# A two-layer network on one core: attention with a shift of 48 and fewer pieces, table sends without an order among themselves, and the last two tiles in two banks

## The chip, the core and the metric

The kernel runs on one core of a Trainium2 chip. The engines of a core work beside one another, each through its own list of instructions in order: TensorE (PE: matrix products; PEld is its weight load), VectorE (DVE), ScalarE (ACT), GpSimd (POOL), and SyncE (SP), which here only issues transfers. Transfers are carried out by the core's DMA engines; SP and GpSimd issue nearly all of them. The metric is the device time of one execution in microseconds (us); the kernel before takes 1606.64 us, the median of three runs (1605.18 to 1611.37).

## The reference, cut to what matters

Two layers work on 2 x 2048 tokens of 256 numbers. The first layer is a gated linear attention beside a quantised product. The second, which the change is about, is a softmax attention with 16 heads of 16 numbers and a bias that falls with distance, beside a layer of 8 experts of which each token goes through two:

```python
slopes = 1.0 / (24.0 ** (1.0 / 8)) ** jnp.arange(1, 9)      # 0.67 down to 0.042
fwd = slopes * jnp.tril(rel) + jnp.triu(neg, 1)             # heads 0..7: keys at or before the query
bwd = slopes * jnp.triu(-rel) + jnp.tril(neg, -1)           # heads 8..15: keys at or after it
scores = jnp.einsum('bhqd,bhkd->bhqk', q, k) / sqrt(16) + bias
out = jnp.einsum('bhqk,bhkd->bhqd', softmax(scores), v) @ Wf + bf
...
pi = _sinkhorn(-logits)                                     # 20 rounds over 8 experts
_, top_idx = jax.lax.top_k(pi, 2)
y = W_down[e] @ (silu(W_gate[e] @ x) * (W_up[e] @ x))       # 256 -> 1024 -> 256
out = sum of y[top_idx[k]] * pi[k] over k                   # x is the normalised row
```

Each head's slope is the same in both directions: heads h and h + 8 have the same one.

## The kernel before

All matrix products are in float32. After the first layer (`layer0`, until 433.7 us of the profiled execution) come two stages, and the change touches both.

**Attention** (`attention`). Keys lie on partitions and queries in columns. Queries come in tiles of 256 (`QT`), keys in tiles of 128. Heads lie in places: four places form a group, whose four heads sit in the four row groups of 32 partitions, so that four small products run beside each other. `PLACES` says which head has which place; groups 0 and 1 hold the forward heads (way 0), groups 2 and 3 the backward ones (way 1). A part is one batch, way, query tile and group, and parts follow one another by batch, then way, then in the order of `ORDERS`, both groups each time. The operands of groups 0 to 3 lie in the buffers `qk0` to `qk3`.

A fixed number, `SHIFT`, takes the place of the row's maximum: it stands as a row of the query operand (`_bias_rows`), so that a score comes out with bias and shift in it and ScalarE takes the exp of it directly. A score without bias is at most 16 (`LIMIT`). A key so far away that 16 less the shift less slope times distance is under -104 has an exp of 0 in float32, and pieces beyond that distance are left out:

```python
reach = math.ceil((104 + LIMIT - SHIFT) / slope) + 1
```

`_units` makes a list of all pieces (one head, one tile of keys, up to 256 queries, widths in multiples of 32) and packs it into units: each of the four row groups is filled up to 512 columns (`WIDE`) with pieces of its head, and goes on to the next part when its own is done, though never more than two parts ahead of the slowest. The loop at the end of `attention` goes through the units. For each it issues the score products (`scores`, L1827), one exp for each row group (L1833), the masks of the diagonal pieces of the unit before (`keep_only`, on VectorE), and the weighted sums of the unit two before (`weighted_sums`, L1847). When a part has ended its sums are copied out of PSUM, and small steps (`normalise`) transpose, divide, project and add; they are taken one in each unit. When a half of 1024 queries is through in both ways, SP stores it to the output (L1819).

**The routing** runs beside it, one step of VectorE work in a unit: the Sinkhorn rounds, the two best experts of every token, and the place of every token in a table in DRAM that is sorted by expert. Then `Routing.sends` writes the table: sixteen times a load of 256 normalised rows and four indirect sends of 128 rows from GpSimd (`Routing.scatter`, L2180). The sends write one tensor, so each waits until the one before has landed. `BEGIN` (32) units before the end of the list the first row loads (`Block.load_rows`, from SP) and weight gathers (L2208, from GpSimd) are issued.

**Experts** (`Experts.pieces`). 32 blocks of 256 rows of the table are computed one after the other. A block's gate and up weights take the room of `qk0`, `qk1` or `qk3` of the attention, its down weights that of `qk2` or of two exp buffers. `open_rows` transposes the rows; for block 0 this is placed four units before the attention ends. `hidden` makes 8 tiles of the 1024 hidden numbers (L2268), and `add_rows` the output of the block: two tiles of 128 rows, 8 products each (L2284), both in one bank of PSUM, then for each tile the weight and bias on VectorE and an indirect send that adds the rows to the output (L2293). These sends write one tensor too and go one after the other. A block's `add_rows` comes one block later, only the last one has nothing behind it.

The order on each engine is not the program's alone: a scheduler places every instruction that has not been held in the program's order by `keep_in_program_order`.

Of the kernel before, what the change touches and what calls it, by code (L numbers as in the profile page):

```python
# [60 lines left out]
ALU = mybir.AluOpType  # L61
# [3 lines left out]
P = 128  # L65
B, N, E = 2, 2048, 256
NT = B * N // P
TPB = N // P
ST = 512
# [5 lines left out]
NG = H1 // 4  # L75


PLACES = (0, 1, 2, 3, 7, 6, 5, 4, 8, 11, 10, 9, 15, 12, 13, 14)
QT = 256

ORDERS = ((6, 7, 2, 3, 0, 1, 4, 5), (1, 0, 5, 4, 7, 6, 3, 2))
WIDE = 512
CENTER = N // 2
NEG_INF = -1.0e9
# [1 line left out]
NFC = FF // P  # L86
# [11 lines left out]
GROWTH, TINY = 1e3, 1e-24  # L98
SPAN = 60.0
LIMIT = 16.0  # L100
SHIFT = 18.0
BEGIN = 32
LATE = 2
KR = HD + 5
# [4 lines left out]
class InOrder:  # L109


    def __init__(self, tc, engine):
        self.tc, self.engine = tc, engine
# [112 lines left out]
@with_exitstack  # L226
def two_layers(ctx: ExitStack, tc: tile.TileContext, a: dict, out: bass.AP):
    nc = tc.nc
    const = ctx.enter_context(tc.tile_pool(name="const", bufs=1))

    def load(name, shape, view=None, eng=None, dt=F32):
        t = const.tile(shape, dt, tag=name, name=name)
        (eng or nc.sync).dma_start(out=t, in_=view if view is not None else a[name])
        return t

    c = SimpleNamespace()
# [24 lines left out]
    c.x_in = a["x"].rearrange("b n e -> (b n) e").rearrange("(t p) e -> p t e", p=P)  # L261
    c.out_v = out[0 : B * N, :].rearrange("(t p) e -> p t e", p=P)

    usual_way(tc, a, out, c)

    def where(flag):
        return tc.If(nc.values_load(flag[0:1, 0:1], min_val=0, max_val=1) > 0)

    with where(c.special):
        with where(c.more):  # L270
            layer1_experts(tc, a, out, c, range(FULLS, NFULL), range(GROUPS, NSMALL // 4))
        with where(c.general):
            general_way(tc, a, out, c)


@with_exitstack
def usual_way(ctx, tc, a, out, c):
    nc = tc.nc
    keep = ctx.enter_context(tc.tile_pool(name="keep", bufs=1))
    acc = keep.tile([P, NT, E], F32, tag="acc", name="acc")  # L280
    la = keep.tile([P, NT, NE], F32, tag="la", name="la")
    norms = keep.tile([P, 1, NSTRIP], F32, tag="norms", name="norms")
    spans = keep.tile([P, NSTRIP, HG, 4, 2], F32, tag="spans", name="spans")
    operands = Operands(nc, keep, a, c)
    ready = Constants(nc, keep, a, c)

    fill = Fill(nc, keep, a, out, c)

    def besides(s):

        if s == 0:
            fill.begin()
            operands.make_first()
            ready.load()
        elif s < NSTRIP - 2:
            fill.rows(s - 1, NSTRIP - 3)
# [7 lines left out]
    routing = Routing(nc, vector, later, a, c)  # L304
    attention(tc, a, out, acc, la, norms, spans, c, operands, ready, routing, vector)


@with_exitstack
def general_way(ctx, tc, a, out, c):
    nc = tc.nc  # L310
    keep = ctx.enter_context(tc.tile_pool(name="gkeep", bufs=1))
    acc = keep.tile([P, NT, E], F32, tag="acc", name="acc")
    xn2T = keep.tile([P, 2, B * N], F32, tag="xn2T", name="xn2T")
    la = keep.tile([P, NT, NE], F32, tag="la", name="la")
    general_layer0(tc, a, acc, xn2T, la, c)
    later = ctx.enter_context(tc.tile_pool(name="glater", bufs=1))
    fill = Fill(nc, later, a, out, c)
    fill.begin()
    fill.rows(0, 1)
    routing = Routing(nc, nc.vector, later, a, c)  # L320
# [1639 lines left out]
class Routing:  # L1960

    def __init__(self, nc, vector, pool, a, c):
        self.nc, self.vector, self.a, self.c = nc, vector, a, c
# [210 lines left out]
    def scatter(self, rows, s):  # L2176

        for n in range(2):
            for to in self.places:
                self.nc.gpsimd.indirect_dma_start(  # L2180
                    out=self.c.table, in_=rows[:, n, :], in_offset=None,
                    out_offset=bass.IndirectOffsetOnAxis(
                        ap=to[:, 2 * s + n : 2 * s + n + 1], axis=0
                    ),
                )

    def sends(self, pool):

# [8 lines left out]
class Block:  # L2197
# [24 lines left out]
    def load_rows(self):  # L2222
# [5 lines left out]
            ),  # L2228
        )
        self.e.tc.keep_in_program_order(load)  # L2230

    def load(self):
        self.load_gate_up()
# [41 lines left out]
            if f % 2:  # L2275
                yield

    def add_rows(self):
        nc, out = self.e.nc, self.e.out
        ps = self.e.rooms("y_ps", self.n, [P, NC * E]).rearrange("p (c d) -> p c d", c=NC)  # L2280
        y = self.e.rooms("y", self.n, [P, NC, E])
        for c in range(self.tiles):
            for fc in range(NFC):
                nc.tensor.matmul(  # L2284
                    ps[:, c, :], lhsT=self.hT[:, fc, c * P : (c + 1) * P], rhs=self.wd[:, fc, :],
                    start=fc == 0, stop=fc == NFC - 1,
                )
        for c in range(self.tiles):
            nc.vector.scalar_tensor_tensor(  # L2289
                y[:, c, :], ps[:, c, :], self.wt[:, c : c + 1], self.e.c.half_bias,  # L2290
                ALU.mult, ALU.add,
            )
            nc.gpsimd.indirect_dma_start(  # L2293
                out=out, out_offset=bass.IndirectOffsetOnAxis(ap=self.to[:, c : c + 1], axis=0),
                in_=y[:, c, :], in_offset=None, compute_op=ALU.add,
            )


class Group:
# [114 lines left out]
class Experts:  # L2414
# [3 lines left out]
    def __init__(self, tc, a, out, c, rooms, blocks, groups):  # L2418
# [5 lines left out]
        for g in groups:  # L2424
# [2 lines left out]
                self.between.append((at, step))  # L2427
            at += 1

    def pieces(self, begun=False):  # L2430


# [20 lines left out]
                between.popleft()[1]()  # L2453
            yield
        if todo:
            todo[-1].add_rows()
        for _, step in between:
            step()

# [181 lines left out]
```

## Time and profile before

| what | value |
|---|---|
| three runs | 1605.18, 1606.64, 1611.37 us |
| the profiled execution: time, span | 1616.2 us, 1614.4 us |
| granted clock of TensorE, mean | 0.987 |
| busy: TensorE, VectorE, ScalarE, GpSimd | 1553.3, 709.9, 689.8, 406.9 us |
| score matmuls, weighted-sum matmuls | 3916 and 3916 |
| exps of the attention (L1833) | 687 |
| sends to the table, first and last start | 64, 611.8 and 842.6 us |
| idle time of GpSimd before them, for a landing | 143.9 us |

The profile is of one execution. Times in it count from its first instruction. A matmul of the program is two in the trace. "Busy" is the time in which an engine has at least one instruction under way; matmuls overlap, so that the start of one burst to the start of the next is the better measure of what a burst costs. In a row of groups there stand line, engine, operation, output and inputs, shapes and count; after the bar the busy time and the mean time of one in ns; after the second bar the engine's idle time before them and what ended it. In a window row there stand the window, its length, for each engine busy time and count, then the granted clock, the DMA engines' share and GB/s.

### The profile page before, as it was taken

The page shows a single profiled execution, that of the slowest core. Times are in us where ns is not written, and L with a number is a line of the kernel's source. Part 1 is how long each engine was busy: PE and PEld are TensorE (multiplying, and loading weights), DVE is VectorE, ACT ScalarE, POOL GpSimd, SP SyncE. Part 2 cuts the span into 40 slices and gives each one's busy share as a digit, 9 for nine tenths or more (in the row PEclk, how much of TensorE's full clock was granted, in tenths as well). Part 3 has the DMA queues.
Part 4 walks back from the last instruction along what each step waited for, and adds up shares of the span by engine and source line. Part 5 has one row for each costly group of instructions (what it writes and reads, how often), then busy time and mean ns, then how long its engine had stood idle before and what let it go on. Part 6 is the DMA issues. An engine that isn't in the chain of part 4 may idle for free.

```text
span 1614.4 us, 32726 instructions
## 1 busy us (share of the span) xinstructions
PE 1553.3 (96%) x13652; PEld 1253.0 (78%) x13652; DVE 709.9 (44%) x2199; ACT 689.8 (43%) x1434; POOL 406.9 (25%) x367
## 2 busy tenths in 40 slices
PE   7789999999999999999999999999999999999995
PEld 4557676676688887887777888888888888888885
DVE  6787776664378867435345222212221221222121
ACT  5454554654586777787877211111121111111110
POOL 4342222212200003234320122232223322232221
PEclk9899999999999999999999999999999999999998
DMA  8810111313450402622215655585756857576521
GB/s 248 216 38 31 55 54 43 94 35 87 143 78 2 85 3 82 145 62 88 79 58 200 245 183 183 183 284 169 240 163 219 258 184 252 166 235 199 174 25 20
DMA packets 84590, 214.19 MB, mean 133 GB/s; under 512 B 8880, under 2 KB 64432, under 8 KB 71984
## 3 DMA queue, kind: packets, MB, share of 16 engines
q0 software_dynamic: 27392, 148.16, 28.9%
q1 hardware_dynamic: 55936, 62.66, 14.5%
q8 instruction: 109, 1.79, 0.5%
q10 hardware_dynamic: 1104, 1.18, 0.2%
q14 instruction: 49, 0.40, 0.1%
HBM read 161.65 MB, written 50.31 MB: 131 GB/s over the span
## 4 chain that ended last, share of the span: by engine, by line
PE 66%; DVE 1%; DMA 0%; issue 0%; ACT 0%; POOL 0%; POOLq 0%
PE h_ps L2268 27%; PE y_ps L2284 14%; PE sc L1827 10%; PE o_ps L1847 9%; PE f_ps L1811 2%; PE o_tr L1784 1%; PE h_ps L2357 1%; PE x_ps L2246 1%; PE on_tr L1803 1%; PE h_ps L2392 0%; DVE pt L117 0%; DMA out<-va,to 0%; DVE o_sb L117 0%; PE h_ps L2380 0%; POOL out L2293 0%
## 5 line engine op out<-in xcount | busy, mean ns | idle before, releaser
L2268 PE MATMUL h_ps<-va,qk 128*128 128x256 f32 x2048 | 448.6, 379 | 0.0
L2268 PEld LDWEIGHTS h_ps<-va,qk 128*128 128x128 f32 x2048 | 388.1, 190 | 57.0 <-issue 4.5
L1833 ACT ACTIVATE pt<-sc 128x512 f32<-128x512 f32 (+3 forms) x687 | 350.5, 597 | 105.1 <-issue 39.7
L2273 ACT ACTIVATE sg<-h_ps 128x256 f32<-128x256 f32 x256 | 98.3, 384 | 530.2 <-PE h_ps L2268 517.0
L2274 DVE TENSOR_TENSOR larger<-sg,h_ps 128x256 f32<-128x256 f32 x256 | 107.9, 421 | 343.7 <-ACT sg L2273 324.6
L1827 PE MATMUL sc<-qk 32*128 32x128 f32 (+6 forms) x3916 | 219.6, 334 | 1.8 <-PE norm_ps L539 1.1
L1827 PEld LDWEIGHTS sc<-qk 32*128 32x128 f32 x3916 | 181.1, 185 | 36.5 <-issue 20.5
L1847 PE MATMUL o_ps<-pt,va 128*32 128x128 f32 (+6 forms) x3916 | 188.6, 319 | 5.9 <-DVE o_sb L117 5.9
L1847 PEld LDWEIGHTS o_ps<-pt,va 128*32 128x32 f32 x3916 | 140.6, 110 | 36.2 <-DVE o_sb L117 7.6
L2293 POOL DMA_INDIRECT out<-va,to x64 | 101.9, 1592 | 182.8 <-DVE larger L2274 55.5
L117 DVE TENSOR_TENSOR pt<-pt,keepmask 128x128 f32<-128x128 f32 (+3 forms) x546 | 118.8, 277 | 61.8 <-ACT pt L1833 61.4
L2284 PE MATMUL y_ps<-qk,larger 128*128 128x256 f32 x512 | 113.8, 379 | 0.1
L2289 DVE SCALAR_TENSOR_TENSOR va<-y_ps,wt,half_bias 128x256 f32<-128x256 f32 x64 | 28.0, 479 | 194.5 <-PE y_ps L2284 194.5
L2284 PE MATMUL y_ps<-larger 128*128 128x256 f32 x512 | 113.2, 379 | 0.0
L2180 POOL DMA_INDIRECT table<-rows,place x64 | 63.3, 989 | 182.5 <-DMA table<-rows,place 143.9
L2284 PEld LDWEIGHTS y_ps<-larger 128*128 128x128 f32 x512 | 96.2, 190 | 12.5
L2284 PEld LDWEIGHTS y_ps<-qk,larger 128*128 128x128 f32 x512 | 95.8, 190 | 12.7 <-DVE larger L2274 0.5
L2208 POOL DMA_INDIRECT qk<-in_wgateup,wrow x32 | 31.7, 989 | 141.3 <-PE h_ps L2268 133.8
L539 PE MATMUL vf_ps<-qk,xnT 128*128 128x512 f32 x128 | 57.9, 605 | 0.0
L117 DVE COPY o_sb<-o_ps 128x256 f32<-128x256 f32 x64 | 26.9, 422 | 51.9 <-PE o_ps L1847 42.7
L539 PEld LDWEIGHTS vf_ps<-qk,xnT 128*128 128x128 f32 x128 | 24.0, 193 | 28.7 <-issue 25.1
L2208 POOL DMA_INDIRECT qk<-in_wdown,wrow x16 | 15.5, 970 | 111.8 <-PE y_ps L2284 71.7
(278 smaller groups left out, 1787.4 us busy)
## 6 DMA issues: line engine op xcount, KB each, us to landing
xb<-table SPq DMA_DIRECT2D x32, 265.0 KB
qk<-qk SPq DMA_DIRECT2D x32, 256.0 KB
qk<-qk SPq DMA_DIRECT2D x64, 128.0 KB
table<-spare SPq DMA_DIRECT2D x3, 2120.0 KB
va<-v SPq DMA_DIRECT2D x4, 1208.0 KB
v<-v SPq DMA_DIRECT2D x8, 574.0 KB
normed<-xn SPq DMA_DIRECT2D x8, 512.0 KB
rows<-normed POOLq DMA_DIRECT2D x16, 256.0 KB
```

The source lines that it names most:

```text
L117: return lambda *a, **k: self.tc.keep_in_program_order(begin(*a, **k))
L539: tc.keep_in_program_order(nc.tensor.matmul(*args, **kwargs))
L1827: nc.tensor.matmul(scs[r][:, at : at + q1 - q0], lhsT=heads[rows, 1, kb * P : (kb + 1) * P], rhs=heads[rows, 0, qt * QT + q0 : qt * QT + q ...
L1833: nc.scalar.activation(pt[:, r, 0:width], scs[r][:, 0:width], AF.Exp)
L1847: nc.tensor.matmul(o_ps[r * HR : (r + 1) * HR, to + q0 : to + q1], lhsT=values[b, way][:, kb, h * VC : h * VC + HR], rhs=pt[:, r, at : at ...
L2180: self.nc.gpsimd.indirect_dma_start(out=self.c.table, in_=rows[:, n, :], in_offset=None, out_offset=bass.IndirectOffsetOnAxis(ap=to[:, 2 * ...
L2208: e.nc.gpsimd.indirect_dma_start(out=w, out_offset=None, in_=e.a[name], in_offset=bass.IndirectOffsetOnAxis(ap=e.c.wrow[:, self.b : self.b ...
L2268: nc.tensor.matmul(ps[:, j, rows], lhsT=self.wgu[:, j, c, f * P : (f + 1) * P], rhs=self.xT[:, c, rows], start=c == 0, stop=c == 1,)
L2273: nc.scalar.activation(sg, ps[:, 0, rows], AF.Silu)
L2274: nc.vector.tensor_tensor(self.hT[:, f, rows], sg, ps[:, 1, rows], ALU.mult)
L2284: nc.tensor.matmul(ps[:, c, :], lhsT=self.hT[:, fc, c * P : (c + 1) * P], rhs=self.wd[:, fc, :], start=fc == 0, stop=fc == NFC - 1,)
L2293: nc.gpsimd.indirect_dma_start(out=out, out_offset=bass.IndirectOffsetOnAxis(ap=self.to[:, c : c + 1], axis=0), in_=y[:, c, :], in_offset= ...
```

## The change

- `SHIFT` goes from 18 to 48, in the query operand and in the reach, which becomes 72 over the slope in place of 102. `PLACES` deals the heads to places anew, and `ORDERS` takes the query tiles in another order. From this `_units` makes another list.
- The sends to the table are declared free of each other: no row is written twice. They are kept in the program's order of issue, and the names are collected; the first row load waits for all of them (`await_rows`).
- `add_rows` is split in `multiply` and `send`. For the last block alone (`apart`) the two tiles go to two banks, and the first tile's weighting and send are issued ahead of the second tile's products.

```diff
-PLACES = (0, 1, 2, 3, 7, 6, 5, 4, 8, 11, 10, 9, 15, 12, 13, 14)
+PLACES = (0, 1, 5, 4, 7, 6, 2, 3, 10, 12, 15, 14, 13, 11, 8, 9)
-ORDERS = ((6, 7, 2, 3, 0, 1, 4, 5), (1, 0, 5, 4, 7, 6, 3, 2))
+ORDERS = ((4, 5, 2, 3, 0, 1, 7, 6), (1, 0, 7, 6, 4, 5, 3, 2))
-SHIFT = 18.0
+SHIFT = 48.0
...
 def scatter(self, rows, s):
         for n in range(2):
             for to in self.places:
-                self.nc.gpsimd.indirect_dma_start(
+                send = self.tc.keep_in_program_order(self.nc.gpsimd.indirect_dma_start(
                     out=self.c.table, in_=rows[:, n, :], in_offset=None,
...
-                )
+                )).ins
+                self.tc.declare_no_dep(send, group=self.group, reason="no row is written twice")
+                self.tc.add_to_no_dep_group(self.group, send)
+                self.c.sent.append(send.name)
...
         self.e.tc.keep_in_program_order(load)
+        self.e.await_rows(load)
...
+    def await_rows(self, load):
+        while self.c.sent:
+            self.tc.add_manual_dep(
+                load.ins, self.c.sent.pop(),
+                mybir.DependencyInfo(mybir.DependencyClass.Sync, mybir.DependencyReason.DATA),
+                reason="the rows of the table that are loaded",
+            )
...
-    def add_rows(self):
+    def add_rows(self, apart=False):
+        tiles = range(self.tiles)
         y = self.e.rooms("y", self.n, [P, NC, E])
+        if apart:
+            parts = [self.e.rooms(name, 0, [P, ST])[:, 0:E] for name in ("h_ps", "y_ps")]
+        else:
+            ps = self.e.rooms("y_ps", self.n, [P, NC * E]).rearrange("p (c d) -> p c d", c=NC)
+            parts = [ps[:, c, :] for c in tiles]
+        for c in tiles:
+            self.multiply(c, parts[c])
+            if apart:
+                self.send(c, parts[c], y)
+        if not apart:
+            for c in tiles:
+                self.send(c, parts[c], y)
...
         if todo:
-            todo[-1].add_rows()
+            todo[-1].add_rows(apart=True)
```

More of the change, by code (lines that the diff above doesn't have):

```diff
@@ L234, in load @@
         return t
-    c = SimpleNamespace()
+    c = SimpleNamespace(sent=[])
     c.ident = load("ident", [P, P])
@@ L303, in usual_way @@
     vector = InOrder(tc, nc.vector)
-    routing = Routing(nc, vector, later, a, c)
+    routing = Routing(tc, vector, later, a, c, "sends")
     attention(tc, a, out, acc, la, norms, spans, c, operands, ready, routing, vector)
@@ L319, in general_way @@
     fill.rows(0, 1)
-    routing = Routing(nc, nc.vector, later, a, c)
+    routing = Routing(tc, nc.vector, later, a, c, "general sends")
     routing.load()
@@ L1960, with __init__ @@
 class Routing:
-    def __init__(self, nc, vector, pool, a, c):
-        self.nc, self.vector, self.a, self.c = nc, vector, a, c
+    def __init__(self, tc, vector, pool, a, c, group):
+        nc = tc.nc
+        self.tc, self.nc, self.vector, self.a, self.c = tc, nc, vector, a, c
+        self.group = group
         self.constants = {
@@ L2276, in hidden, with multiply, send @@
                 yield
-    def add_rows(self):
-        nc, out = self.e.nc, self.e.out
-        ps = self.e.rooms("y_ps", self.n, [P, NC * E]).rearrange("p (c d) -> p c d", c=NC)
+    def add_rows(self, apart=False):
+        tiles = range(self.tiles)
         y = self.e.rooms("y", self.n, [P, NC, E])
[L2282 to L2291, printed above, removed]
-            )
[L2293 to L2296, printed above, removed]
+        if apart:
[10 more added lines that the diff above has]
+                self.send(c, parts[c], y)
+    def multiply(self, c, ps):
+        for fc in range(NFC):
+            self.e.nc.tensor.matmul(
+                ps, lhsT=self.hT[:, fc, c * P : (c + 1) * P], rhs=self.wd[:, fc, :],
+                start=fc == 0, stop=fc == NFC - 1,
+            )
+    def send(self, c, ps, y):
+        nc = self.e.nc
+        nc.vector.scalar_tensor_tensor(
+            y[:, c, :], ps, self.wt[:, c : c + 1], self.e.c.half_bias, ALU.mult, ALU.add
+        )
+        nc.gpsimd.indirect_dma_start(
+            out=self.e.out, in_=y[:, c, :], in_offset=None,
+            out_offset=bass.IndirectOffsetOnAxis(ap=self.to[:, c : c + 1], axis=0),
+            compute_op=ALU.add,
+        )
 class Group:
@@ L2428, in __init__ @@
             at += 1
+    def await_rows(self, load):
[4 more added lines that the diff above has]
+                reason="the rows of the table that are loaded",
+            )
     def pieces(self, begun=False):
```

## The prediction

> **What bounds the kernel now.** I read the stage windows first: the projections before the first score matmul, the attention from there to its last weighted sum, the experts to their last matmul, and the tail.
>
> ```profile
> core 0: us, PE busy (x) PEld busy (x) DVE busy (x) ACT busy (x) POOL busy (x), PEclk, DMA share, GB/s
> 433.70:892.90 459.20, 451.91 (x8193) 369.76 (x8193) 269.21 (x987) 352.76 (x690) 97.37 (x123) 1.00 0.33 87
> 892.90:1598.10 705.20, 705.08 (x3489) 606.97 (x3488) 154.21 (x439) 121.78 (x297) 188.24 (x149) 1.00 0.60 191
> ```
>
> TensorE is busy 451.9 of the attention's 459.2 us and all of the experts' 705 us, at the full granted clock (1.00). ScalarE, which takes the exps, is next with 352.8 us. The table of waits then says whether TensorE waits for anybody in the attention:
>
> ```profile
> PE o_ps L1847 <- DVE o_sb L117: 5.9, 8, 1.5
> PE sc L1827 <- PE norm_ps L539: 1.1, 1, 1.1
> PE sk_ps L1578 <- ACT pt L1833: 0.4, 2, 0.2
> PE sc L1827 <- ACT pt L1833: 0.4, 1, 0.4
> ```
>
> Those four rows come to 7.8 us. So the attention lasts as long as its matmuls do. Its rhythm stands in the timeline of TensorE (start, time, engine and line, count): a burst of scores for one unit, then a burst of weighted sums for the unit two before it.
>
> ```profile
> 656.56 1.26 PE L1827 MATMUL sc<-qk 32*128 32x128 f32 x20
> 657.74 1.07 PE L1847 MATMUL o_ps<-pt,va 128*32 128x128 f32 x22
> 658.74 1.26 PE L1827 MATMUL sc<-qk 32*128 32x128 f32 x22
> 659.93 1.07 PE L1847 MATMUL o_ps<-pt,va 128*32 128x128 f32 x20
> 660.93 1.32 PE L1827 MATMUL sc<-qk 32*128 32x128 f32 x26
> 662.18 1.07 PE L1847 MATMUL o_ps<-pt,va 128*32 128x128 f32 x20
> ```
>
> From one score burst to the next it is 2.18 and 2.19 us: 1.18 to 1.25 for scores, 1.00 for sums. ScalarE needs less: in the same stretch twelve exps of 512 columns take 6.40 us, 2.13 for a unit's four. Last, the chain of work at the end (start, time, what), and then GpSimd's timeline:
>
> ```profile
> 1591.13 6.92 PE y_ps L2284 x32
> 1598.07 0.49 DVE va L2289
> 1598.83 3.78 DMA out<-va,to
> 1603.65 1.26 POOL out L2293
> ```
>
> The second output send waits until the first has landed. And every send to the table waits for the one before it:
>
> ```profile
> 839.65 0.97 POOL L2180 DMA_INDIRECT table<-rows,place  x1 [2.23 <-DMA table<-rows,place]
> 842.61 0.97 POOL L2180 DMA_INDIRECT table<-rows,place  x1 [1.99 <-DMA table<-rows,place]
> 879.37 1.01 POOL L2208 DMA_INDIRECT qk<-in_wdown,wrow  x1 [33.16 <-PE sc L1827]
> ```
>
> The first two of these rows are the last sends to the table; the third gathers the down weights of the first block, once TensorE has released their room.
>
> **Part 1: fewer pieces.** The list that `_units` makes can be counted from its code. Reach falls from 102 to 72 over the slope, so with the new deal there are 153 units for 175, 1786 pieces for 1958 and 299,520 columns for 346,880. The old count agrees with the trace, which has 3916 score matmuls, two for a piece. I price the two bursts of a unit by their start-to-start times in the trace, which sum to 214.7 us for scores and 177.5 us for sums.
>
> Sums: 177.5/175 = 1.014 a unit, whatever the number of pieces (1.013 where the busiest row group has three, 1.021 where it has five). 153 units make 155.2, so 22.3 us go.
>
> Scores depend on how many pieces the busiest row group has: three 1.17 us (122 units), four 1.26 (40), five 1.64 (13, two long stalls among them). The new list has 75, 57 and 21 such units: 87.9 + 71.9 + 34.4 = 194.1 us. So 20.6 go, and not the 27.0 of 22 average bursts; the smaller pieces give 6.4 back. Together -42.9.
>
> The rest of TensorE's stage (459.2 - 214.7 - 177.5 = 67.0 us: transposes, output projection, router) stays, count for count.
>
> The rows of single matmuls by columns (mean ns after the bar) show what a small piece saves:
>
> ```profile
> L1847 PE MATMUL o_ps<-pt,va 128*32 128x128 f32 x1456 | 144.1, 278 | 0.0
> L1847 PE MATMUL o_ps<-pt,va 128*32 128x64 f32 x304 | 35.9, 226 | 3.2 <-DVE o_sb L117 3.2
> L1847 PE MATMUL o_ps<-pt,va 128*32 128x32 f32 x100 | 10.1, 197 | 0.0
> ```
>
> 128 to 64 columns is worth 52 ns, 64 to 32 another 29: still straight, with no floor at 64. This matters because pieces of 32 columns go from 50 to 120. The Trainium skill, page "TensorEngine Tiling (Array Packing)", section "Instruction Overhead", says that a matmul has an overhead of about 60 cycles and that one of a single column takes as long as one of 60. By that rule 70 more pieces of 32 would each be charged 28 columns too many in four matmuls; at the 0.84 ns a column of the experts' stream (64 matmuls of 256 columns in 13.81 us), that is an estimate of at most 6.6 us, and the sum would be about 39.8 and not 46.4. The row from 64 to 32 speaks against it.
>
> ScalarE drops from 687 exps to 597, off the path. VectorE's masks go from 546 to 554; their cover is its own idle 190 us of the stage. It fails where many masks meet, since the sums two units later wait for them: the ten slowest score bursts and six slow sum bursts are 12 us longer together than the usual ones, and several stand at units with 8 to 12 masks (one row: twelve masks, 2.42 us at 617.1). Both lists have thirteen units with eight or more, the longest 12 before and 11 now. My averages carry these stalls along at about their present size; bounds: all gone (-12) or doubled (+12).
>
> **Part 2: sends not ordered.** The 64 sends run from 611.8 to 843.6 us, 3.6 each, and 143.9 us of GpSimd's idle time is their waiting for one another. They are on no path now: the first experts' rows are loaded at 845.7, and TensorE transposes them at 884.1, 8.7 before the stage ends. Pulled in by 42.9, that transpose would stand at 841; ordered rows would land at about 842.6 + 3.1 to the load + 3.8 as an output send takes = 849.5, 8.5 late. Unordered, a step of four costs 4 x (0.99 + 0.30) plus 1.2 for the next rows, about 6.4; sixteen end near 715. I take 0; the ends are 0 and +8.5. The new wait on all sends sits on SP's queue ahead of the first row load; behind it are the output stores of batch 1 and later row loads, and at 715 none of them is due. The gate and up gathers behind the sends then wait for heads 0 and 1, whose last scores are at unit 117, near 750, a hundred before they are used.
>
> **What moves closer.** Down weights of block 0 go into the room of way 1's first group. That group's last score now stands in the last but one unit, with 4.9 us of the stage left (0.3 + 1.0 + 0.9 + 2.75 of the bursts behind it); before, the gather was issued at 879.4, 13.5 us before the end. TensorE needs it at 896.8 - 892.9 = 3.9 after the end. So 8.7 us are left from release to use. No row shows this gather land; the nearest are the output send with 3.78 for an eighth of its bytes, and the use itself, 17.5 after issue, which did not wait. At the 367 to 421 GB/s of the loads from 883 to 890 us, 1 MB is 2.6, so I estimate 3.8 + 2.6 = 6.4 and take 0; the bounds are 0 and 17.5 - 8.7 = +8.8.
>
> **Part 3: last two tiles in two banks.** The first tile's 16 matmuls end 3.46 us earlier than both (half of 6.92). Its send goes out 0.8 after that, as now, at 4.3 after the start of y_ps in place of 7.7; the second still waits for its landing and goes out 4.5 later, at 8.8. It is ready itself at 6.92 + 0.8 = 7.7. So the end moves by 3.5. If the first send took as long as the one at 1586.5 (4.9 from issue to issue), it would be 3.1; if landing didn't matter, 4.6.
>
> **Sum.** -42.9 - 3.5 = -46.4. The profiled execution took 1616.2 us (span 1614.4), 9.6 above the median of the runs shown, 1606.64; I leave that distance as it is. 1606.6 - 46.4 = 1560.2.
>
> **The rivals.**
> - The stalls double, or a wait takes their place (masks, or the down weights at the hand-over): 12 us back, 1572. For it: bursts differ more from row group to row group, and two gathers sit closer to their use. Against it: TensorE waited only 7.8 us in 459.
> - Stalls thin out with the units: 1560.2 - 12 = 1548. For it: the longest queue of masks shrinks. Against it: the router's own VectorE work in the first 70 units stays.
> - Pieces under 64 columns cost what 64 do. 70 more of 32, two matmuls each in scores (272 ns in place of 244) and sums (226 in place of 197): 70 x 2 x 57 ns = 8 us at most, 1568. Against it are those rows, which still fall.
> - ScalarE becomes the bound. 153 x 2.13 = 326 us against a stage of 416, so it does not decide. The change then does nothing only if the units weren't TensorE's time at all: 1606. Against it is the 2.18 rhythm, whose two bursts leave no gap.
> - Slower: the table. TensorE's transpose of the first rows holds everything behind it. It would stand at 841, and would have to be kept until 841 + 46 = 887 to lose the whole gain. With the 6.9 from a last send to its rows that is (880 - 612)/63 = 4.3 us a send, more than the ordered 3.6; at 5 us a send the rows would come at 934 and the time would be 1560 + 93 = 1653. For it: single waits of 6.4 us when other loads share the queue. Against it: nothing in the new order makes a send wait for the last.
>
> **How the numbers follow.** Forecast (1553 to 1567) 0.67, stalls or hand-over 0.15, small pieces 0.05, thinner stalls 0.07, no effect 0.03, slower by the table 0.03. I predict 1560. The range reaches to both stall cases: 1547 to 1575. About 0.5%, 8 us, is what a measurement can tell from no change; so faster 0.94, same 0.03, slower 0.03.
>
> **What would show it.** Right: the attention window ends near 850 with TensorE still busy over 97%; 3572 score matmuls and 597 exps; sends to the table about 1.3 apart, ended near 715; row loads and gate gathers long before 841; the experts' window still 705; two output sends some 4.5 apart, the first during y_ps. Wrong: new rows of TensorE waiting for VectorE's masks or a DMA, score bursts above 1.27 on average, sends that still wait, or a row load after 841.

## The result and the profile after

The changed kernel took 1567.65 us (median of four runs, 1562.31 to 1569.72) against 1608.64 us for the kernel before (four runs, 1605.18 to 1611.37): a ratio of 0.9741 with an interval of 0.9707 to 0.9776. The forecast was 1560, with a range of 1547 to 1575. But the same program, measured a second time (experiment `r1_after_again`), took 1624.47 us where the kernel before took 1613.33. This section reads the first measurement; most of the experiments are about the second.

The stage windows of the changed kernel (attention, experts up to the first of the last two tiles, the rest), with the columns of the prediction's windows:

```profile
436.50:850.20 413.70, 409.89 (x7509) 339.91 (x7509) 268.79 (x995) 305.01 (x600) 99.58 (x124) 1.00 0.35 94
850.20:1550.90 700.70, 700.64 (x3471) 603.57 (x3471) 154.53 (x439) 121.52 (x297) 187.27 (x149) 1.00 0.60 193
1550.90:1567.50 16.60, 3.36 (x16) 2.62 (x14) 0.92 (x2) 0.00 (x0) 3.12 (x2) 0.66 0.15 21
```

The attention went from 459.2 to 413.7 us, TensorE still busy 99% of it at the full granted clock. The start-to-start times of the bursts split this into scores 190.7 (214.7 before), sums 155.4 (177.5) and the rest 67.6 (67.0). The 16 matmuls of the second of the last two tiles stand in the third row; with them the experts last 704.1 us, for 705.2 before. The table of waits, TensorE's rows inside the attention (total, times, longest; the same four as in the prediction):

```profile
PE o_ps L1847 <- DVE o_sb L117: 1.8, 3, 0.8
PE sc L1827 <- PE norm_ps L539: 1.1, 1, 1.1
PE sk_ps L1578 <- ACT pt L1833: 0.5, 2, 0.3
PE sc L1827 <- ACT pt L1833: 0.5, 1, 0.5
```

These rows come to 3.9 us, for 7.8 before; two more, not there before, hold 0.7. GpSimd's timeline shows the sends going out without a wait for a landing ("issue": the engine waited for nothing that the profile shows), and later the gathers of the first block's down weights:

```profile
681.06 0.97 POOL L2182 DMA_INDIRECT table<-rows,place  x1 [0.30 <-issue]
682.34 0.97 POOL L2182 DMA_INDIRECT table<-rows,place  x1 [0.30 <-issue]
683.61 1.03 POOL L2182 DMA_INDIRECT table<-rows,place  x1 [0.30 <-issue]
...
844.38 0.94 POOL L2213 DMA_INDIRECT qk<-in_wdown,wrow  x1 [2.47 <-PE sc L1827]
845.62 0.95 POOL L2213 DMA_INDIRECT qk<-in_wdown,wrow  x1 [0.30 <-issue]
```

And the end, first the chain, then GpSimd's last two output sends:

```profile
1547.36 3.47 PE h_ps L2303 x16
...
1551.61 3.74 DMA out<-va,to
1556.38 1.27 POOL out L2313
```

```profile
1551.61 1.56 POOL L2313 DMA_INDIRECT out<-va,to  x1 [7.88 <-DVE va L2310]
1556.10 1.55 POOL L2313 DMA_INDIRECT out<-va,to  x1 [2.93 <-DMA out<-va,to]
```

The first tile's sixteen matmuls stand at 1547.36 by themselves, its send follows 4.25 us after their start, and the second send 4.49 later: the prediction had 4.3 and 4.5. From the last weighted sum to the end of the span it is 717.3 us, for 721.5 before.

### The profile page after: what moved, and what is told of

It reads as the page before. It is cut to its first block, busy times and chain, and to the rows that moved or that the text cites. A ratio compares the mean times of both kernels' runs of the same rounds, so it can differ in the third digit from the quotient of the medians.

```text
span 1567.5 us, 31245 instructions
## 1 busy us (share of the span) xinstructions
PE 1513.8 (97%) x12964; PEld 1224.2 (78%) x12964; DVE 710.0 (45%) x2207; ACT 641.6 (41%) x1344; POOL 408.1 (26%) x367
## 4 chain that ended last, share of the span: by engine, by line
PE 64%; DVE 1%; DMA 0%; issue 0%; ACT 0%; POOL 0%; POOLq 0%
PE h_ps L2274 28%; PE y_ps L2303 14%; PE sc L1827 9%; PE o_ps L1847 7%; PE f_ps L1811 2%; PE h_ps L2378 1%; PE o_tr L1784 1%; PE x_ps L2252 1%; PE on_tr L1803 0%; PE h_ps L2413 0%; DVE pt L117 0%; DMA out<-va,to 0%; PE h_ps L2303 0%; PE h_ps L2401 0%; ACT pt L1833 0%
## 5 line engine op out<-in xcount | busy, mean ns | idle before, releaser
L1833 ACT ACTIVATE pt<-sc 128x512 f32<-128x512 f32 (+2 forms) x597 | 302.8, 596 | 106.3 <-issue 51.7
L1827 PE MATMUL sc<-qk 32*128 32x256 f32 (+6 forms) x3572 | 198.4, 328 | 1.6 <-PE norm_ps L539 1.1
L1827 PEld LDWEIGHTS sc<-qk 32*128 32x128 f32 x3572 | 167.8, 185 | 31.3 <-ACT pt L1833 14.5
L1847 PE MATMUL o_ps<-pt,va 128*32 128x256 f32 (+6 forms) x3572 | 164.4, 310 | 2.0 <-DVE o_sb L117 1.8
L1847 PEld LDWEIGHTS o_ps<-pt,va 128*32 128x32 f32 x3572 | 123.7, 109 | 28.2 <-issue 4.8
L2303 PE MATMUL y_ps<-larger 128*128 128x256 f32 x496 | 109.7, 379 | 0.0
L2335 POOL DMA_INDIRECT acc<-in_wgateup,wpart x16 | 15.4, 961 | 109.4 <-DMA xb<-table 88.0
L218 POOL TENSOR_TENSOR mx_r<-mx_r,mx_pw 128x512 f32<-128x512 f32 x17 | 21.6, 1271 | 83.7 <-DVE mx_r L217 57.6
```

The source lines that it names most:

```text
L1827: nc.tensor.matmul(scs[r][:, at : at + q1 - q0], lhsT=heads[rows, 1, kb * P : (kb + 1) * P], rhs=heads[rows, 0, qt * QT + q0 : qt * QT + q ...
L1833: nc.scalar.activation(pt[:, r, 0:width], scs[r][:, 0:width], AF.Exp)
L1847: nc.tensor.matmul(o_ps[r * HR : (r + 1) * HR, to + q0 : to + q1], lhsT=values[b, way][:, kb, h * VC : h * VC + HR], rhs=pt[:, r, at : at ...
L2303: self.e.nc.tensor.matmul(ps, lhsT=self.hT[:, fc, c * P : (c + 1) * P], rhs=self.wd[:, fc, :], start=fc == 0, stop=fc == NFC - 1,)
```

## The experiments

Every kernel below is the changed kernel but for its edit, and is timed against the kernel before on its own chip. The four groups ran on four chips.

**Group 1: the parts taken back one at a time.** The kernel before: 1613.25 us (1608.84 to 1614.4).

Old deal of the heads, and with it 166 units in place of 153:

```diff
-PLACES = (0, 1, 5, 4, 7, 6, 2, 3, 10, 12, 15, 14, 13, 11, 8, 9)
-ORDERS = ((4, 5, 2, 3, 0, 1, 7, 6), (1, 0, 7, 6, 4, 5, 3, 2))
+PLACES = (0, 1, 2, 3, 7, 6, 5, 4, 8, 11, 10, 9, 15, 12, 13, 14)
+ORDERS = ((6, 7, 2, 3, 0, 1, 4, 5), (1, 0, 5, 4, 7, 6, 3, 2))
```

> The changed kernel with PLACES and ORDERS as they were before; SHIFT stays 48. The pieces hold the same 299,520 columns, but the list has 166 units and not 153 (1818 pieces; the busiest row group has 2 to 3 pieces in 84 units, 4 in 63, 5 in 19). Theory (the stage costs its units, and a score burst its busiest row group): sums 166 x 1.014 = 168.3, scores 84 x 1.17 + 63 x 1.26 + 19 x 1.64 = 208.8, the rest 67, so 444 us of attention in place of 413.7: about 30 slower than the changed kernel, 1597 us. Rival (the stage costs its columns, the deal is worth nothing): 1568 us.

Old shift with the new deal, 173 units:

```diff
-SHIFT = 48.0
+SHIFT = 18.0
```

> The changed kernel with SHIFT 18 again, in the new deal and order. 173 units, 1952 pieces, 346,880 columns (busiest row group: 3 pieces in 108 units, 4 in 51, 5 in 14). Theory by units: sums 175.4, scores 126.6 + 64.3 + 22.9 = 213.8, the rest 67, so 456 us of attention against 459 before the change; with the tail of 3.5, about 1609 less 6, 1603 us. Rival (the deal is a gain of its own, whatever the shift, as large as with 48): 13 units less than before, 1580 us.

Sends in order again:

```diff
-                self.tc.declare_no_dep(send, group=self.group, reason="no row is written twice")
-                self.tc.add_to_no_dep_group(self.group, send)
```

> The changed kernel with the sends to the table ordered again. The first send stood at 624.3 us in the changed kernel; 63 more at the 3.66 us of before end at 855, and the rows land some 6.9 after the last begins, at 862, while TensorE transposed them at 840.5. Theory (the order was hidden before and would not be now): TensorE stands still for some 20 us ahead of that transpose, 1588 us. Rival (hidden anyway, for instance since the sends wait less than before): 1568 us.

Last two tiles in one bank:

```diff
-            todo[-1].add_rows(apart=True)
+            todo[-1].add_rows()
```

> The changed kernel with the last block's two tiles in one bank again. Theory: the first output send goes out 7.7 us after the last products begin in place of 4.4, the second 12.3 in place of 8.9, and the end comes 3.4 us later: 1571 us, and the same in the chain at the end. Rival (the landing of the sends sets the end whatever their start, or another transfer ends last): within 0.5 us of the changed kernel.

| kernel | time, us | range | ratio to before (interval) |
|---|---|---|---|
| `e1_old_deal` | 1643.93 | 1642.39 to 1647.42 | 1.0196 (1.0173 to 1.0219) |
| `e2_old_shift` | 1654.90 | 1653.57 to 1656.70 | 1.0261 (1.0241 to 1.0281) |
| `e3_ordered_sends` | 1598.01 | 1591.87 to 1604.46 | 0.9916 (0.9890 to 0.9943) |
| `e4_one_bank` | 1632.42 | 1631.26 to 1634.23 | 1.0126 (1.0107 to 1.0145) |

No theory had this. Three of four came 47 to 61 us above what the units and the tail account for; the kernel whose sends are ordered came 10 above its 1588. So something that goes with unordered sends cost some 50 us here and nothing in the first measurement.

The ordered kernel did show the late rows that were expected of it. TensorE's timeline, then SP's:

```profile
840.08 0.66 PE L1784 MATMUL o_tr<-ident,o_sb 128*128 128x128 f32 x4
862.41 1.09 PE L2250 MATMUL x_ps<-ident,xb 128*128 128x128 f32 x4 [21.67 <-DMA xb<-table]
863.43 2.09 PE L1827 MATMUL sc<-qk 32*128 32x256 f32 x22
865.45 1.94 PE L1847 MATMUL o_ps<-pt,va 128*32 128x96 f32 x30
```

```profile
849.08 1.21 SPq L2227 DMA_DIRECT2D xb<-table  x2
```

The last send starts at 846.3, the row load is issued at 849.08, and the transpose that TensorE could have done at 840.74 is done at 862.41: 21.67 us of waiting. The bursts behind it take 2.09 and 1.94 us in place of some 1.2 and 1.07; the granted clock is half for 23.9 us from 843.8, most of which falls into the wait. The list of matmuls is that of the first measurement, so the two traces can be matched matmul by matmul: the stage is 31.0 us longer, 2.7 of it at its start (the clock is half from 434.2 to 441.0), 1.7 up to the wait, 21.7 of waiting and 4.9 behind it. Of the 10 us between 1598 and 1588, some 5 may be the chip's: the kernel before takes 1613.25 us on it, for 1608.64.

**Group 2: is it the program, or where it runs?** The kernel before: 1613.33 us (1608.11 to 1617.31). The first kernel is the changed one without an edit, the second is `e4_one_bank` again:

> The changed kernel itself once more, beside the next three on one chip. In the three runs with free sends (old deal, old shift, one bank) TensorE issued less than half of its matmuls while the sends went out, 900 in 104 us where the changed kernel had issued 1969, with waits that end in issue and a granted clock of 0.83; with ordered sends it did not. Theory A (it hangs on the chip or the load on which a program runs; the changed kernel is as liable as the others): about 1630 us here if the chip is like the last one. Theory B (it hangs on the program, on where its instructions lie against the sends): 1568 us again.

> The kernel with one bank for the last two tiles again, on this chip. Theory A: within 5 us of the changed kernel on this chip, whichever that is, 3.4 above it. Theory B: 1632 us as before, whatever the changed kernel does.

The third was meant to let the sends go in pairs only, by a group for each tile:

```diff
+                group = f"{self.group} {s} {n}"
-                self.tc.declare_no_dep(send, group=self.group, reason="no row is written twice")
-                self.tc.add_to_no_dep_group(self.group, send)
+                self.tc.declare_no_dep(send, group=group, reason="no row is written twice")
+                self.tc.add_to_no_dep_group(group, send)
```

> The changed kernel with the sends free only in pairs: the two of one tile of rows are free of each other, each pair waits for what came before it. At 1.3 us for the second issue and about 3.7 for a landing a pair takes 5 us, 32 of them 160: from 624 to about 784, before the rows are wanted at 840. Theory (TensorE is starved of instructions by many sends under way at once): the 104 us of slow issue are gone on any chip, 1568 us. Rival (any sends closer than the ordered ones starve it, or it is not the sends at all): as slow as the changed kernel on this chip.

The fourth has only the free sends: old `PLACES`, `ORDERS`, `SHIFT` and one bank.

> The kernel before with the free sends alone: SHIFT 18, old deal and order, one bank. By the prediction's step the sends are on no path, so the time is that of before, 1609 us. Rival (free sends starve TensorE, as in the three runs): some 60 us slower than before, 1670 us, with the loss between the first send and the last.

| kernel | time, us | range | ratio to before (interval) |
|---|---|---|---|
| `r1_after_again` | 1624.47 | 1622.20 to 1629.53 | 1.0078 (1.0049 to 1.0107) |
| `r2_one_bank_again` | 1632.88 | 1632.83 to 1632.93 | 1.0120 (1.0087 to 1.0154, two runs) |
| `r3_pairs` | 1624.33 | 1621.59 to 1628.38 | 1.0065 (1.0040 to 1.0090) |
| `r4_sends_only` | 1660.64 | 1658.06 to 1666.50 | 1.0304 (1.0271 to 1.0338) |

The program is the same and the time is 57 us longer: none of the five executions is near the four of the first measurement. Freeing the sends alone costs 47.3 us (1660.64 - 1613.33). The place is the stretch in which the sends go out: matched matmul by matmul, `r1_after_again` is not behind the first measurement at 620.8, is 58.5 us behind at 733.1, and ends the attention 60.1 behind. First measurement, from the first send to the end of the last; then the waits of TensorE there (the view gives no row), and the DMA queues there (packets, MB, share):

```profile
624.30:728.60 104.30, 104.15 (x1971) 86.93 (x1970) 61.79 (x254) 79.17 (x156) 79.95 (x103) 1.00 0.57 159
```

```profile
q0 software_dynamic: 4064, 11.96, 38.2%
q1 hardware_dynamic: 3632, 4.38, 17.9%
q8 instruction: 15, 0.25, 1.1%
```

The same three views of the same program in `r1_after_again`:

```profile
618.60:719.60 101.00, 85.66 (x925) 54.46 (x923) 30.68 (x131) 36.01 (x69) 77.91 (x103) 0.82 0.60 163
```

```profile
PE o_ps L1847 <- issue: 6.3, 16, 0.9
PE sc L1827 <- issue: 5.5, 10, 1.0
```

```profile
q0 software_dynamic: 4064, 11.96, 40.8%
q1 hardware_dynamic: 3632, 4.38, 18.3%
q8 instruction: 7, 0.11, 0.5%
```

The sends go out equally fast (64 in 101 and 104 us), the two data queues carry the same packets to the byte, and TensorE issues 925 matmuls where it issued 1971. Its idle time ends in "issue": no semaphore held it. The idle time is only 15 us of the loss, because single matmuls that come far apart count as busy. Over the rest of the attention the two runs go at nearly the same speed, 17.9 and 17.7 matmuls a us.

Queue 8 carries instructions, in packets of 16 KB (104 of them in the whole execution, with 12,964 matmuls). Fewer came in the slow stretch, 7 for 15, about as many fewer as matmuls: 132 and 131 matmuls for each packet. That looks as if TensorE had been starved of instructions, and the expectations of these groups call it so. But the trace speaks against it. The seven packets begin after the same number of matmuls as the same seven packets of the first measurement, six of them to within 13 matmuls and the seventh 72 sooner, and take no longer (0.9 to 1.6 us, for 0.9 to 1.5). So TensorE had as much fetched ahead as in the run that was not slowed, and the packets were fewer because it used them up more slowly. Nor does it ever run dry: packets begin 4.4 to 17.5 us apart, and it never goes longer than 1.1 us without beginning a matmul or a weight load. It trickles. Between the packets at 660.02 and 675.73 its timeline in `r1_after_again` has:

```profile
663.33 0.62 PE L1847 MATMUL o_ps<-pt,va 128*32 128x256 f32 x6
664.24 1.88 PE L1847 MATMUL o_ps<-pt,va 128*32 128x128 f32 x13 [0.29 <-issue]
666.43 0.27 PE L1847 MATMUL o_ps<-pt,va 128*32 128x128 f32 x1 [0.31 <-issue]
667.13 0.40 PE L1847 MATMUL o_ps<-pt,va 128*32 128x128 f32 x2 [0.44 <-issue]
```

In the first measurement such a burst goes through in one row, 26 to 28 matmuls in 1.08 us. What spaces TensorE's instructions out here, no row names.

The pairs settled nothing by themselves. What ended the idle time ahead of the sends in `r3_pairs`, and in the ordered `e3_ordered_sends`:

```profile
DMA table<-rows,place: 7.5, 4
```

```profile
DMA table<-rows,place: 137.6, 61
```

Four waits for 61: the edit left the sends practically free, 1.7 us apart on average (1.6 without it), and TensorE at 10.8 matmuls a us (1195 in the 110.5 us of the sends). Its time is that of a free kernel, not of one with two sends under way.

**Group 3: does the distance of the sends decide?** The kernel before: 1613.12 us (1607.83 to 1615.12). GpSimd clears an unread tile after each send, or after each of the first 32 only:

```diff
                 self.c.sent.append(send.name)
+                pause = pool.tile([P, 1024], F32, tag="pause", name="pause", bufs=1)
+                self.tc.keep_in_program_order(self.nc.gpsimd.memset(pause, 0.0))
```

> The changed kernel with one addition: after each of the 64 sends GpSimd clears a tile of 128x1024 that nobody reads (0.96 us in a row of the changed kernel's profile), so that sends still do not wait for one another but start some 2.3 us apart in place of 1.3. They would run from 624 to about 624 + 64 x 2.3 + 16 x 1.2 = 790, ahead of the first rows' transpose at 840. Theory, it is how densely they come: at 2.3 apart TensorE's instructions arrive in time, as they do at 3.5 apart with ordered sends. Then TensorE issues 18 to 19 matmuls a us throughout, and the time is 1568 plus at most 4 whichever chip this is. Rival, what starves TensorE is any send that does not wait for the last, at whatever distance: the window of the sends shows 9 to 12 matmuls a us, and the time is 1620 or more (longer than the 1624 of the changed kernel's second measurement if the starving lasts as long as the sends). If this chip is one on which the changed kernel is not starved, both give 1568, and the kernel with half of its sends paced, run beside this one, tells so.

> The changed kernel with the clearing of a tile behind the first 32 sends only; the last 32 come 1.3 us apart as in the changed kernel. One program on one chip then has both distances. Theory, density: TensorE keeps 18 to 19 matmuls a us while the first half goes out (about 624 to 708) and falls to 9 to 12 in the second (about 708 to 760); half of the 57 us is lost, 1596. Rival, any unordered send: it falls to 9 to 12 from the first send on, and the time is 1620 or more. If neither half is starved, this chip is like that of the first measurement: 1570.

All paced: 1580.53 us (1575.6 to 1583.06), ratio 0.9793 (0.9760 to 0.9826). Half paced: 1609.77 us in one run. The half-paced kernel holds both cases in one execution. Its windows: the paced half of the sends, the start of the free half, and its half-clock stretch; then the queues of the paced and of the free half (623 to 700 and 700 to 750 us):

```profile
623.00:700.00 77.00, 72.58 (x1324) 60.37 (x1322) 46.40 (x170) 53.30 (x105) 69.90 (x83) 0.96 0.55 136
700.00:750.00 50.00, 41.37 (x422) 27.92 (x422) 14.33 (x60) 16.74 (x33) 40.60 (x55) 0.78 0.39 126
...
700.70:710.90 10.20, 8.15 (x111) 5.71 (x106) 1.25 (x6) 3.97 (x8) 8.13 (x11) 1.00 0.42 133
711.00:724.70 13.70, 11.62 (x121) 9.11 (x121) 6.10 (x29) 3.94 (x8) 11.54 (x16) 0.50 0.41 129
```

```profile
q8 instruction: 10, 0.16, 1.0%
...
q8 instruction: 3, 0.05, 0.5%
```

17.2 matmuls a us while the sends come 2.4 us apart on average, 8.4 while they come 1.5 apart. How busy the DMA engines are doesn't decide it: their share is 0.55 (136 GB/s) in the half that isn't slowed and 0.39 (126 GB/s) in the half that is. The slowing begins with the first free sends, at 700.7, and it begins at the full clock: 111 matmuls in 10.2 us at 1.00. The half clock comes only at 711, so it follows the slowing and does not start it. Matched with the first measurement, the attention is 44.2 us longer: 32.6 in the free half (28 were expected), 7.0 in the paced half, 2.7 and 1.8 at the stage's start and end.

The fully paced kernel is 13 us above the first measurement, its attention 14.3. Matched in the same way, 2.7 of the 14.3 are at the stage's start, where the clock is half from 436.2 to 443.0, and 7.0 stand where the paced half of the other kernel has its 7.0, around a wait for VectorE. Two rows of VectorE's timeline in the fully paced kernel, and the row of TensorE's waits that follows from such rows:

```profile
638.12 1.73 DVE L117 CAST nowhere<-nowhere_f 128x4 int32<-128x4 f32 x1
638.20 1.68 DVE L117 TENSOR_SCALAR part<-row 128x32 f32<-128x32 f32 x1
```

```profile
PE o_ps L1847 <- DVE o_sb L117: 8.2, 6, 4.4
```

A cast of four columns takes 1.73 us beside the clearing of the tile, where it takes 0.31 in the changed kernel. The Trainium skill, page "SBUF — State Buffer", section "Who interferes with whom", says that a copy, cast or tensor_scalar in a two-port mode and a GpSimd instruction lock each other out for the whole instruction. The trace agrees as to the ends: this cast ends at 639.85 and the clearing beside it at 639.84, and the next small operations, ahead of the following clearing, take 0.2. It does not show why the cast, begun 0.74 us ahead of that clearing's row, was not through by then.

**Group 4: a pause that holds nobody.** The kernel before: 1607.13 us (1605.71 to 1611.79). The pause becomes a power of four columns; in the second kernel the shift goes to 64 as well, with a deal searched for it (143 units, 1644 pieces):

```diff
-                self.tc.keep_in_program_order(self.nc.gpsimd.memset(pause, 0.0))
+                self.tc.keep_in_program_order(
+                    self.nc.gpsimd.tensor_tensor(pause, one, self.c.expo, ALU.pow)
+                )
...
-SHIFT = 48.0
+SHIFT = 64.0
-PLACES = (0, 1, 5, 4, 7, 6, 2, 3, 10, 12, 15, 14, 13, 11, 8, 9)
-ORDERS = ((4, 5, 2, 3, 0, 1, 7, 6), (1, 0, 7, 6, 4, 5, 3, 2))
+PLACES = (2, 1, 4, 3, 6, 7, 0, 5, 13, 9, 15, 14, 11, 12, 8, 10)
+ORDERS = ((6, 7, 2, 3, 1, 0, 4, 5), (0, 1, 5, 4, 7, 6, 3, 2))
```

> The changed kernel with a pause after each send again, but the pause is a power of 128x4 (1.04 us in the projections' rows) in place of the clearing of 128x1024. The first paced kernel lost 14.3 us of attention against the changed kernel's first measurement (428.0 for 413.7). Theory, most of that is VectorE: beside the clearings its small casts took 1.73 us in place of 0.31 (nowhere, 128x4), o_sb came late and TensorE waited 4.4 us for it, and the clock dropped for 6.8 us. A power of four columns does not hold VectorE, so the wait for o_sb falls back to under 2 us in all and the time to 1568 to 1573. Rival, the loss is what is left of the starving at 2.1 to 2.3 us a send: then it stays at about 1580 with TensorE idle for issue or at a lower clock inside 625 to 775 us.

> The kernel paced by powers, with 64 subtracted in place of 48 and the heads dealt anew for it: 143 units for 153, 1644 pieces for 1786. By the changed kernel's prices (1.014 a unit for sums; scores 1.17, 1.26 and 1.64 a unit where the busiest row group has three, four and five pieces, of which there are 66, 66 and 9, and two units with two at 1.1) scores fall from 194.1 to 177.4 and sums by 10.1: 26.8 less than the kernel paced by powers, about 1543 if that gives 1570. The sends end near 775, the first rows are then transposed near 815, so nothing is late. Rival, with fewer units in front of it something that was hidden comes on the path (the first expert block's weights, wanted by 390 us of attention in place of 414): the attention falls, and TensorE waits between it and the experts; less than half of the 26.8 is kept.

`p2_paced_pow`: 1564.52 us (1564.19 to 1568.62), ratio 0.9735 (0.9709 to 0.9761). `b1_shift_64`: 1539.90 us (1538.57 to 1545.07), ratio 0.9571 (0.9548 to 0.9594), the fastest of all. The cast in the first, and the attention window of each, with a wait of the second:

```profile
629.87 0.17 DVE L117 CAST nowhere<-nowhere_f 128x4 int32<-128x4 f32 x1
```

```profile
430.90:845.00 414.10, 409.95 (x7509) 339.94 (x7510) 268.11 (x995) 305.06 (x600) 171.40 (x188) 1.00 0.35 94
```

```profile
434.20:823.50 389.30, 386.32 (x6941) 319.26 (x6941) 263.10 (x975) 270.22 (x542) 171.91 (x186) 0.99 0.36 95
```

```profile
PE y_ps L2309 <- DMA qk<-in_wdown,wrow: 2.1, 1, 2.1
```

With the power the cast is at 0.17 and the attention at 414.1, that of the first measurement. The wait for `o_sb` fell from 8.2 to 2.4 us (under 2 was expected) and the half clock of 6.8 us inside the sends is gone: 5.8 + 3.4 = 9.2 of the 13.9 us by which the two profiled attentions differ (428.0 and 414.1). Another 2.7 is the half clock at the start. By the ratios of the timed runs the two paced kernels differ by 9.4 us (0.0058 of 1613). The powers also set the sends further apart, 2.60 us on average for 2.35, and no run separates the two. With 143 units the attention lost another 24.8 of the 26.8 us priced, scores 13.9 (191.1 to 177.2, where the price said 177.4) and sums 10.7 (155.3 to 144.6). The wait that the rival named is there, behind the attention, but it is 2.1 us.

Open: on the chip of this last group no kernel ran whose sends are 1.3 us apart, so it isn't shown that TensorE would be slowed there; that pacing ends the slowing rests on group 3.

## Why the prediction was right, and where it was not

**Fewer pieces: right.** Sums were priced at 155.2 and took 155.4. Scores, priced at 194.1 by the pieces of the busiest row group, took 190.7, so the table was 3.4 too dear. The term that was off is the 1.64 us of units with five pieces: the 21 of them took 1.47 each, since where the 13 of before had two long stalls (3.93 and 2.05 us) these have one (1.97). Of the attention's 45.5 us the prediction had 42.9. The Trainium skill's rule of about 60 cycles a matmul (page "TensorEngine Tiling (Array Packing)", section "Instruction Overhead") left no trace: after the change the rows of sums by 128, 64 and 32 columns stand at 277, 224 and 198 ns, still falling, and scores and sums together came 3.2 below their price, not 6.6 above. The same table forecast `b1_shift_64` to 2 us. The two kernels meant to split the gain between shift and deal did not split it: against `e4_one_bank` on their chip, with 2.8 us for the bank, `e1_old_deal` is 14.3 us slower and `e2_old_shift` 25.3, which is 15 and 10 short of their expectations (1597 and 1603, for 1567.65), and all three are slowed for 100 us of their list, each in another part of it. What is left standing is the count of units, by which neither does much alone: 173 with the deal alone, 166 with the shift alone, 153 with both, 175 before.

**Stalls carried along: only in part.** The rival of thinner stalls came about halfway. Behind the first score burst, which is long in both lists, the nine slowest took 9.1 us more together than nine median bursts before, and 3.1 more after. The waits inside the attention fell from 7.8 to 4.6 us.

**Sends: the step "I take 0" held once and failed on the chips of groups 1 to 3.** That the forecast came out is luck in this: where `r1_after_again` ran, the same program lies outside its range. In the first measurement they ran 624.3 to 728.6, nobody waited for them, and only the end was off (715 forecast), because the start was 12.5 late. Elsewhere the same step is worth +47 (`r4_sends_only`) and the time stands 57 above the first measurement's. What the step left out: it asked who waits for the sends' data, and the slower rival ("the table") asked only when the rows arrive. Neither asked what a denser stream of sends does to an engine that waits for none of them. Its mechanism could not have been read from the profile before; that the DMA engines would about double their share while the sends go out (0.30 from 611.8 to 843.6 before, 0.57 from 624.3 to 728.6 after) could, but that share is not what decides (group 3).

**Ordered sends, bound +8.5: too small.** `e3_ordered_sends` waited 21.7 us, and lost 4.9 more behind the wait. The last send began 3.7 later than before the change (846.3 for 842.6), and from the issue of the row load to the transpose it was 13.3 us and not 3.8, 9.5 more. A price from one output send was no price for a load of 265 KB among others.

**Hand-over of the down weights: right, with less to spare than thought.** The gather was issued at 844.38 and used at 853.27, 8.9 us later (8.7 forecast), without a wait. The estimate of 6.4 us for its landing was low: in `b1_shift_64` TensorE used the weights 8.3 us after the first gather's issue and had waited 2.1 for them. If it lands as late in the changed kernel, 0.6 of the 8.9 are left.

**Tail: right.** 3.5 us forecast. `e4_one_bank` and `r2_one_bank_again` have 720.7 us from the last weighted sum to the end, `r1_after_again` 717.9: 2.8. The timed difference of 8.4 between the last two is larger: 4.1 are in their slowed attention (477.9 and 473.8) and 1.6 ahead of it, which no run explains.

**From profile to median: this made the 7.6 us of the miss.** The profiled executions moved from 1616.2 to 1569.3, 46.9 for a sum of 46.4. That the two agree so well is partly luck: the attention lost 45.5 and what follows it 4.2, 49.7 in all, and the first layer, which the change does not touch, came out 2.8 longer (436.5 us for 433.7). The medians moved 41.0. The prediction left the profiled execution's distance to the median at 9.6 us; after the change it was 1.7. The profiled execution of before was slower than any of the four timed runs, and the changed kernel's was not, so the distance did not carry over.

## What to carry to other kernels

Before you free transfers from one another, ask also what the denser stream does to engines that wait for none of them. On three chips TensorE got through half of its work while free sends came 1.5 to 1.6 us apart; where they came 2.4 us apart and were just as free, it got through nearly all of it. So it was their distance, not their order, that had to be kept. Look for such a loss in the work done per us: the waits and the busy share showed only a part of it. And when a queue of instruction packets goes quiet, compare where in the instruction list each packet begins before you say that the engine was starved: here the packets only followed the engine. Put a pause between sends beside which the neighbours' small operations stay short, and let sends stay well ahead of their use. Measure a change that packs traffic more than once and on more than one chip, since one measurement can show a gain that the next takes back.

## What was not expected of the hardware

- With sends of 128 rows of 1060 bytes 1.6 us apart on average, TensorE did 9.2 matmuls a us in place of 18.9. At 2.4 to 2.6 us apart it did 17.2 to 18.7, at 3.5 apart (`e3_ordered_sends`, 4019 in 218 us) 18.4. Shown, within one execution of `h1_half_paced` and between it and the fully paced kernel on the same chip: the rate goes with the distance. Shown in `r1_after_again`: the instruction packets were not late, TensorE paused at most 1.1 us at a time, and no semaphore held it. Shown in `h1_half_paced`: it was slowed at the full clock too. Not shown: what holds it.
- Whether it happens differs between measurements of one program (18.9 and 9.2 with the same traffic). It did on three chips with free sends and not in the first measurement; what differs between the chips, or their state, is open.
- Half-clock stretches came after TensorE had begun to stand still or to slow: at 711.0 in `h1_half_paced`, whose dense sends begin at 700.7, and from 843.8 for 23.9 us in `e3_ordered_sends`, whose wait begins at 840.74. Others have nothing to do with the sends, such as that at the start of the attention (434.2 to 441.0 in `e3_ordered_sends`, none there in the first measurement).
